# The last expert layer of a gated block: the routed tiles dealt out over three weight buffers by thirds of the sorted list

## The chip, the cores and the metric

The kernel runs on one core of a Trainium2 chip. The metric is the device time of one execution in microseconds (us). The kernel before was timed three times: the median is 1126.99 us, the lowest 1126.54 us and the highest 1131.32 us.

## The reference: what is computed

Four sequences of 512 tokens, 512 features each, run through two gated layers. Each adds an attention-like term and then an expert layer to the residual. All is done in float32. The change touches only the last of the four parts, the second layer's mixture of experts:

```
logits = x @ router_w.T                      # 2048 tokens, 8 experts
topk_w, topk_idx = top_k(softmax(logits), 2) # two experts for each token
out_e  = (silu(x @ gate_w[e]) * (x @ up_w[e])) @ down_w[e]   # 512 -> 352 -> 512
result = sum over the two chosen e of weight * out_e  +  shared expert (704 wide)
x = x + tanh(g_ffn[1]) * result              # x here is layer-normed on the way in
```

The router picks 2 of 8 experts for each of 2048 tokens, so there are 4096 (token, expert) rows. The inputs are fixed by their seed. The reference's own choice of experts gives 551, 523, 549, 483, 478, 438, 454 and 620 rows for experts 0 to 7.

## The kernel before, in words

The kernel does first layer attention, 32 small experts over 48 tiles, second layer attention, and then the part that matters here. All of it is one function, `flamingo_gated`.

**The sorted list.** In the last layer the 4096 rows are sorted by expert. Each expert's rows are padded to whole tiles of 128 rows (`P`). With the counts above that is 5, 5, 5, 4, 4, 4, 4 and 5 tiles, 36 in all, and `NTS` is 36. `NT4` is 39, the most that any routing could need; the last three would run inside a conditional (line 1537) if more than 36 were used. `tile_i` (line 935) is a small table that says which tile of the sorted list is done at which step; before the change it is simply 0, 1, 2, and so on. From it VectorE works out, for each step, the expert (`eid`, lines 1358 to 1360), the rows of the weight table to fetch (`wrow`), and the column of the slot table where the step's tokens stand (`column`, `pick4`).

**Three weight buffers.** `wbuf` holds `NW = 3` buffers. Step i uses the buffer `at4[i] % 3`, so steps i, i+3, i+6 share one. `weights4(i)` (line 1393) fetches the gate and up weights, 128 rows of 2816 floats (1.44 MB), and the down weights, 128 rows of 1536 floats (0.79 MB), with two indirect DMAs that GpSimd issues. Before it, line 1367 compares the experts of step i and step i-3:

```
V.tensor_tensor(same[:, NW:NTS], eid[:, NW:NTS], eid[:, : NTS - NW], ALU.is_equal)
...
V.scalar_tensor_tensor(wrow, same, float(4 * E1 * P), eid, ALU.mult, ALU.add)
```

Where they agree, the row numbers are pushed out of bounds, and the DMA moves nothing: the weights are in the buffer already.

**One step.** `rows4` gathers a tile's 128 token rows (steps 0 to 3), `in4` turns them with a ScalarE copy `x32` (line 1441), four TensorE transposes (line 245) and a ScalarE copy into `xrT` (line 246). From step 4 on, `pair_rows4` gathers two tiles at once into `rp`; 16 DMAs on SyncE's queue rearrange them into `q` (line 1453), and VectorE transposes them (`in4_blocks`, line 1461). `up4` does gate and up on TensorE (`pgr`, `pur`, line 1472), Silu on ScalarE (1474) and the product on VectorE (1475). `turn4` transposes the product (`pti`, 1483) and ScalarE copies it (`itr`, 1484 and 1485). `down4` does the down projection (`por`, 1492), VectorE adds half the bias (`yr`, 1494), and GpSimd scatters the rows to DRAM (1495).

**The order.** TensorE and VectorE follow the order in which the program is written (`by_hand`). TensorE's is: up(i+1), then the transposes of tile i+2 where step i+2 is below 4, then down(i), then `pti`(i+1). GpSimd, ScalarE and SyncE are ordered by the planner that compiles the kernel. After step i the program asks for `weights4(i + 3)`. The weights of steps 0 and 1 are asked for earlier (line 1398), while the shared expert of the same layer (`d1`, lines 1203 to 1229, whose weights lie in the buffer that step 2 will use) is still at work. The third, `weights4(2)`, is written after `up4(0)` and after the gathers of `pair_rows4` for tiles 4 to 7.

**After the loop.** The second part of the shared expert follows, one step of it ahead of the last down projection, and the results go out.

Of the kernel before, what the change touches and what calls it, by code (L numbers as in the profile page):

```python
# [34 lines left out]
NT4 = (2 * T + E1 * (P - 1)) // P  # L35
NTS = 2 * T // P + E1 // 2
# [6 lines left out]
NW = 3  # L43
# [22 lines left out]
def flamingo_gated(  # L66
# [9 lines left out]
    V, A, G, PE = nc.vector, nc.scalar, nc.gpsimd, nc.tensor  # L76
# [42 lines left out]
    for g in range(B):  # L119
# [23 lines left out]
        pattern=[[1, P]], channel_multiplier=-1,  # L143
# [97 lines left out]
    def transposed(dst, src, name, part=slice(0, P)):  # L241

        pt = ps_t.tile([P, DC, P], F32, name=name, tag="pt")
        for c in range(DC):
            PE.transpose(pt[:, c, :], src[:, c * P : (c + 1) * P], ident)
        A.copy(dst, pt[:, :, part])  # L246
# [15 lines left out]
    ENG = mybir.EngineType  # L262
# [441 lines left out]
    def views4(w):  # L704
        wgu = wbuf[w % NW][:, :WROW].rearrange("p (a c i) -> p a c i", a=2, c=DC)
        return wgu, wbuf[w % NW][:, WROW:].rearrange("p (c d) -> p c d", d=D)
# [7 lines left out]
    def load_shared4(u, w):  # L714
        wgu, wd = views_s4(u, w)
        nc.sync.dma_start(out=wgu, in_=(wsgu1a, wsgu1b)[u])
        nc.sync.dma_start(out=wd[:, 0:2, :], in_=wsd1[u * IS[0] :, :][: 2 * P, :].rearrange("(c p) d -> p c d", p=P))
        if u == 0:
            for h in range(2):
                nc.sync.dma_start(out=wd[h * N : (h + 1) * N, 2, :], in_=wsd1[2 * P : IS[0], :])  # L720
# [134 lines left out]
    for i in range(NT2):  # L855
# [4 lines left out]
        k = i // 4 + 2  # L860
# [50 lines left out]
    for i in range(2):  # L911
        for k in range(2):
# [3 lines left out]
                pattern=[[(g2 - g) * P, 2], [TB * P, TB]], base=1 + k * T + g * P, channel_multiplier=1,  # L916
# [15 lines left out]
    for c in range(2, DC):  # L932
        G.tensor_tensor(fold, fold, ident[:, 32 * c : 32 * c + E1], ALU.add)
    tile_i = c4.tile([P, NT4], I32, name="tile_i")
    G.iota(tile_i, pattern=[[1, NT4]], base=0, channel_multiplier=0)


    stats4 = [c4.tile([P, 3, TB], F32, name=f"st4_{g}") for g in range(B)]
# [303 lines left out]
    def step(gen, n=1):  # L1242
        for _ in range(n):
            next(gen)
# [135 lines left out]
    def gather(out_, src, idx, n):  # L1380
        G.indirect_dma_start(
            out=out_,
            out_offset=None,
            in_=src[:, :],
            in_offset=bass.IndirectOffsetOnAxis(ap=idx, axis=0),
            bounds_check=n - 1,
            oob_is_err=False,
        )
# [4 lines left out]
    def weights4(i):  # L1393
        wgu, wd = views4(at4[i])
        gather(wgu.rearrange("p a c i -> p (a c i)"), wgu1, wrow[:, i : i + 1], E1 * P)
        gather(wd.rearrange("p c d -> p (c d)"), wd1, wrow[:, i : i + 1], E1 * P)
# [37 lines left out]
    def rows4(i):  # L1434
        xrs[i] = work.tile([P, D], F32, name=f"xr{i}", tag="row", bufs=NROW)
        gather(xrs[i], h4_dram, gat4[:, i : i + 1], T)

    def in4(i):
        xrTs[i] = work.tile([P, DC, P], F32, name=f"xrT{i}", tag="xnT", bufs=3)
        x32 = work.tile([P, DC, B4, 32], F32, name=f"x32_{i}", tag="row", bufs=NROW)  # L1440
        A.copy(x32, xrs.pop(i).rearrange("p (r c d) -> p c r d", r=B4, c=DC))
        transposed(xrTs[i], x32.rearrange("p c r d -> p (c r d)"), f"ptr{i}")
# [3 lines left out]
    def pair_rows4(i):  # L1446
        rp = d4.tile([P, 2, D], F32, name=f"rp{i}", tag="rp", bufs=3)
        for j in range(2):
            gather(rp[:, j, :], h4_dram, gat4[:, i + j : i + j + 1], T)
        q = d4.tile([P, 2, B4, P], F32, name=f"q{i}", tag="q", bufs=2)  # L1450
        for a in range(B4):
            for r in range(DC):
                nc.sync.dma_start(
                    out=q[32 * r : 32 * r + 32, :, a, :], in_=rp[32 * a : 32 * a + 32, :, r * P : (r + 1) * P]
                )
        for j in range(2):
            xqs[i + j] = q[:, j]
# [8 lines left out]
    def up4(i):  # L1466
        (wgu, _), xbT = views4(at4[i]), xrTs.pop(i)
        pg = ps.tile([P, I1], F32, name=f"pgr{i}", tag="g")
        pu = ps.tile([P, I1], F32, name=f"pur{i}", tag="u")
        for a, p_ in enumerate((pg, pu)):  # L1470
            for c in range(DC):
                PE.matmul(p_, lhsT=xbT[:, c, :], rhs=wgu[:, a, c, :], start=(c == 0), stop=(c == DC - 1))  # L1472
        sg = work.tile([P, 512], F32, name=f"sgr{i}", tag="sg")
        A.activation(sg[:, :I1], pg, AF.Silu)
        V.scalar_tensor_tensor(sg[:, :I1], pu, slots[:, 1, i : i + 1], sg[:, :I1], ALU.mult, ALU.mult)  # L1475
        sgs[i] = sg

    def turn4(i, tag="it"):
        pt = ps_t.tile([P, 3, P], F32, name=f"pti{i}", tag="pt")
        it = work.tile([P, 3, P], F32, name=f"itr{i}", tag=tag)  # L1480
        sg = sgs.pop(i)
        for ic, (i0, ni) in enumerate(chunks):
            PE.transpose(pt[:ni, ic, :], sg[:, i0 : i0 + ni], ident)
        A.copy(it[:, 0:2, :], pt[:, 0:2, :])
        A.copy(it[: I1 - 2 * P, 2, :], pt[: I1 - 2 * P, 2, :])
        its[i] = it

    def down4(i):
        (_, wd), it = views4(at4[i]), its.pop(i)
        po = ps.tile([P, D], F32, name=f"por{i}", tag="o")  # L1490
        for ic, (i0, ni) in enumerate(chunks):
            PE.matmul(po, lhsT=it[:ni, ic, :], rhs=wd[:ni, ic, :], start=(ic == 0), stop=(ic == 2))  # L1492
        yr = work.tile([P, D], F32, name=f"yr{i}", tag="row", bufs=NROW)
        V.tensor_tensor(yr, po, half_db, ALU.add)  # L1494
        d = G.indirect_dma_start(  # L1495
            out=y4_dram[:, :],
            out_offset=bass.IndirectOffsetOnAxis(ap=put4[:, i : i + 1], axis=0),
            in_=yr,
            in_offset=None,
            bounds_check=2 * T - 1,  # L1500
            oob_is_err=False,
        )

        tc.declare_no_dep(d.ins, group="y4", reason="rows are distinct")
        tc.add_to_no_dep_group("y4", d.ins)

    after = [shared4(1, W5, g, wd2) for g in range(B)]
    BYPE = 4
    for i in range(BYPE):
        rows4(i)  # L1510
    for i in range(BYPE, BYPE + 4, 2):
        pair_rows4(i)
    in4(0)
    up4(0)
    weights4(NW - 1)
    in4(1)
    turn4(0)
    for i in range(NTS):
        if i + 1 < NTS:
            up4(i + 1)  # L1520
        if i + 2 < NTS:
            (in4 if i + 2 < BYPE else in4_blocks)(i + 2)
        if i % 2 == 0 and BYPE + 4 <= i + 6 < NTS:
            pair_rows4(i + 6)
        if i + 1 == NTS:
            step(after[0])
        down4(i)
        if i + NW < NTS:
            weights4(i + NW)
        elif i + NW == NTS:  # L1530
            load_shared4(1, W5)
        if i + 1 < NTS:
            turn4(i + 1)
    step(after[0], 3)
    by_hand.close()

# [109 lines left out]
```

## Time and profile before

| what | value |
| --- | --- |
| median of three runs | 1126.99 us |
| the profiled execution: own time | 1132.97 us |
| the profiled execution: span, first to last instruction | 1131.2 us |
| TensorE busy | 1016.3 us, 90% of the span |
| mean granted TensorE clock | 0.946 |
| routed steps, first gate matmul to the last step's gate matmul | 711.98 to 992.58 us |
| instructions in the span | 11060 |

The profiled execution is one run and not the median one: its own time is 1132.97 us, of which 1131.2 us are its span, so that 1.8 us lie around the span. Times in the views are from the start of the span. In a timeline a row gives the start, the busy time, the engine, the line, the operation with output and inputs and its count, and in brackets the idle time just before it with what ended that time. PE is TensorE's matmul, ACT is ScalarE, DVE is VectorE, POOL is GpSimd, and SPq is SyncE's DMA queue.

### The profile page before, as it was taken

The page shows a single profiled execution, that of the slowest core. Times are in us where ns is not written, and L with a number is a line of the kernel's source. Part 1 is how long each engine was busy: PE and PEld are TensorE (multiplying, and loading weights), DVE is VectorE, ACT ScalarE, POOL GpSimd, SP SyncE. Part 2 cuts the span into 40 slices and gives each one's busy share as a digit, 9 for nine tenths or more (in the row PEclk, how much of TensorE's full clock was granted, in tenths as well). Part 3 has the DMA queues.
Part 4 walks back from the last instruction along what each step waited for, and adds up shares of the span by engine and source line. Part 5 has one row for each costly group of instructions (what it writes and reads, how often), then busy time and mean ns, then how long its engine had stood idle before and what let it go on. Part 6 is the DMA issues. An engine that isn't in the chain of part 4 may idle for free. (4 is left out here: it accounts for less than half of the span.)

```text
span 1131.2 us, 11060 instructions
## 1 busy us (share of the span) xinstructions
PE 1016.3 (90%) x3334; PEld 495.0 (44%) x3334; DVE 466.1 (41%) x1244; ACT 212.1 (19%) x461; POOL 375.2 (33%) x412
## 2 busy tenths in 40 slices
PE   4479889999999999799486798899999999999998
PEld 2144434444444444334243444555555555544443
DVE  5989936322232322376856353122222222218111
ACT  1143111222222222023232300211111111110000
POOL 2001142334322340466624443554554544310000
PEclk8689889999999999899878599999999999999999
DMA  9522136688888786765633606697799878639100
GB/s 323 220 75 80 44 85 234 220 296 270 283 288 268 257 289 223 261 174 173 200 93 124 57 1 169 194 294 221 244 322 319 271 274 281 216 111 325 38 37 37
DMA packets 88477, 223.12 MB, mean 197 GB/s; under 512 B 21054, under 2 KB 38494, under 8 KB 80224
## 3 DMA queue, kind: packets, MB, share of 16 engines
q0 software_dynamic: 28608, 107.81, 30.3%
q1 hardware_dynamic: 57504, 110.40, 28.4%
q10 hardware_dynamic: 2304, 4.20, 1.5%
q8 instruction: 27, 0.44, 0.2%
q14 instruction: 34, 0.28, 0.1%
HBM read 206.16 MB, written 35.57 MB: 214 GB/s over the span
## 5 line engine op out<-in xcount | busy, mean ns | idle before, releaser
L788 PE MATMUL gu<-wbuf,xbT 128*128 128x512 f32 (+1 forms) x512 | 176.7, 602 | 0.9 <-ACT xbT L246 0.7
L950 POOL DMA_INDIRECT yk<-y_dram,rows_of x76 | 83.8, 1102 | 107.2 <-DVE x L967 51.2
L1472 PE MATMUL pgr<-wbuf,xrT 128*128 128x352 f32 x288 | 93.9, 470 | 11.8 <-DMA wbuf<-in_wgu_dram,wrow 8.7
L770 POOL DMA_INDIRECT xb<-h_dram,get x48 | 48.1, 1001 | 168.5 <-issue 96.9
L788 PEld LDWEIGHTS gu<-wbuf,xbT 128*128 128x128 f32 (+1 forms) x512 | 64.2, 165 | 79.4 <-issue 78.3
L1492 PE MATMUL por<-wbuf,itr 128*128 128x512 f32 (+1 forms) x216 | 98.6, 592 | 0.0
L795 DVE SCALAR_TENSOR_TENSOR sgb<-gu,xb,sgb 128x256 f32<-128x256 f32 (+1 forms) x64 | 30.9, 484 | 160.9 <-ACT sgb L793 136.7
L1475 DVE SCALAR_TENSOR_TENSOR sgr<-pur,slots,sgr 128x352 f32<-128x352 f32 x36 | 21.0, 583 | 177.7 <-PE pur L1472 126.1
L813 PE MATMUL pob<-wbuf,itb 128*128 128x512 f32 (+1 forms) x256 | 91.2, 599 | 0.0
L1472 PE MATMUL pur<-wbuf,xrT 128*128 128x352 f32 x288 | 91.1, 459 | 0.0
L1203 PE MATMUL pg<-lnT,wbuf 128*128 128x512 f32 (+1 forms) x224 | 86.0, 563 | 0.1
L1203 PE MATMUL pu<-lnT,wbuf 128*128 128x512 f32 (+1 forms) x224 | 79.6, 532 | 1.9 <-DVE it L1209 1.9
L1495 POOL DMA_INDIRECT y_dram<-yr,put x36 | 36.8, 1021 | 114.5 <-DVE yr L1494 106.0
L1472 PEld LDWEIGHTS pgr<-wbuf,xrT 128*128 128x128 f32 x288 | 52.7, 193 | 38.4 <-DVE yr L1494 9.1
L1472 PEld LDWEIGHTS pur<-wbuf,xrT 128*128 128x128 f32 x288 | 54.7, 190 | 30.5
L1219 PE MATMUL po<-wbuf,it 128*128 128x512 f32 x128 | 63.0, 627 | 4.2 <-DVE x L1229 3.3
L1492 PEld LDWEIGHTS por<-wbuf,itr 128*128 128x128 f32 (+1 forms) x216 | 41.0, 190 | 41.9 <-issue 34.7
L748 POOL DMA_INDIRECT found<-cnt_dram,look x48 | 48.3, 1006 | 26.3 <-issue 14.3
L1203 PEld LDWEIGHTS pg<-lnT,wbuf 128*128 128x128 f32 (+1 forms) x224 | 36.1, 185 | 46.3 <-issue 44.5
L1203 PEld LDWEIGHTS pu<-lnT,wbuf 128*128 128x128 f32 (+1 forms) x224 | 34.9, 175 | 42.8 <-issue 38.1
L1209 DVE SCALAR_TENSOR_TENSOR it<-pu,ub_sb,sg 128x512 f32<-128x512 f32 (+1 forms) x24 | 16.9, 703 | 85.9 <-PE pu L1203 65.3
L818 DVE COPY y<-pob 128x512 f32<-128x512 f32 x48 | 33.2, 691 | 44.7 <-PE pob L813 31.2
(397 smaller groups left out, 1288.8 us busy)
## 6 DMA issues: line engine op xcount, KB each, us to landing
wbuf<-in_wgu_dram SPq DMA_DIRECT2D x32, 1024.0 KB
wbuf<-in_wd_dram SPq DMA_DIRECT2D x32, 512.0 KB
y_dram<-y SPq DMA_DIRECT2D x48, 256.0 KB
q<-rp SPq DMA_DIRECT2D x256, 32.0 KB
y<-y_dram SPq DMA_DIRECT2D x32, 256.0 KB
lnT<-in_xT_dram SPq DMA_DIRECT2D x4, 1024.0 KB
x<-in_x_dram SPq DMA_DIRECT2D x16, 256.0 KB
h_dram<-h SPq DMA_DIRECT2D x16, 256.0 KB
```

The costliest lines, as they stand in the source:

```text
L748: G.indirect_dma_start(out=found[k][:, j, :], out_offset=None, in_=cnt_dram[:, :], in_offset=bass.IndirectOffsetOnAxis(ap=look2[:, i : i + ...
L770: G.indirect_dma_start(out=rows0[i], out_offset=None, in_=h_dram[:, :], in_offset=bass.IndirectOffsetOnAxis(ap=get2[:, i : i + 1], axis=0) ...
L788: PE.matmul(gu[p_, :], lhsT=xbT[:, c, p_], rhs=weights[e][0][:, c, :], start=(c == 0), stop=(c == DC - 1),)
L795: V.scalar_tensor_tensor(sg[p_, :I0], gu[p_, I0:], xb[p_, D + e : D + e + 1], sg[p_, :I0], ALU.mult, ALU.mult)
L813: PE.matmul(po[p_, :], lhsT=it[:, ic, p_], rhs=weights[e][1][:, ic, :], start=(ic == 0), stop=(ic == I0 // P - 1),)
L818: V.tensor_copy(y, po)
L950: G.indirect_dma_start(out=yk, out_offset=None, in_=y_dram[:, :], in_offset=bass.IndirectOffsetOnAxis(ap=rows_of[:, t, k : k + 1], axis=0) ...
L1203: PE.matmul(p_[m, :n], lhsT=wgu[:, a, c, i], rhs=lnT[g][:, c, k], start=(c == 0), stop=(c == DC - 1))
L1219: PE.matmul(po, lhsT=it[:, ic, k * P : (k + 1) * P], rhs=wd[:, ic, :] if ic < 2 else wd2, start=(ic == 0), stop=(ic == 2),)
L1472: PE.matmul(p_, lhsT=xbT[:, c, :], rhs=wgu[:, a, c, :], start=(c == 0), stop=(c == DC - 1))
L1492: PE.matmul(po, lhsT=it[:ni, ic, :], rhs=wd[:ni, ic, :], start=(ic == 0), stop=(ic == 2))
L1495: d = G.indirect_dma_start(out=y4_dram[:, :], out_offset=bass.IndirectOffsetOnAxis(ap=put4[:, i : i + 1], axis=0), in_=yr, in_offset=None, ...
```

## The change

The table `tile_i` no longer counts 0, 1, 2 and so on. Its first 36 entries are filled as a 12 by 3 block whose entry (k, w) is k + 12 w. Step 3k + w therefore does tile 12 w + k of the sorted list: the first buffer walks through tiles 0 to 11, the second through 12 to 23, the third through 24 to 35. The last three entries, of the conditional, stay 36 to 38, and take a second small instruction.

Besides this, the gathers of `pair_rows4` for tiles 4 to 7 are written after `weights4(2)`, not before `in4(0)`. And ScalarE and GpSimd follow the written order from `in4(0)` until the end of step 1 (`in_order`); afterwards the planner orders them, as before. Where such a stretch falls among instructions of the same engine that are written outside it is still the planner's choice.

```diff
-    G.iota(tile_i, pattern=[[1, NT4]], base=0, channel_multiplier=0)
+
+    G.iota(
+        tile_i[:, :NTS].rearrange("p (k w) -> p k w", w=NW), pattern=[[1, NTS // NW], [NTS // NW, NW]],
+        base=0, channel_multiplier=0,
+    )
+    G.iota(tile_i[:, NTS:], pattern=[[1, NT4 - NTS]], base=NTS, channel_multiplier=0)
@@
     for i in range(BYPE):
         rows4(i)
-    for i in range(BYPE, BYPE + 4, 2):
-        pair_rows4(i)
+    in_order = ExitStack()
+    in_order.enter_context(tc.manual_schedule(engines={ENG.Activation, ENG.Pool}))
     in4(0)
     up4(0)
     weights4(NW - 1)
+    for i in range(BYPE, BYPE + 4, 2):
+        pair_rows4(i)
     in4(1)
     turn4(0)
     for i in range(NTS):
@@
         if i + 1 < NTS:
             turn4(i + 1)
+        if i + 3 == BYPE:
+            in_order.close()
     step(after[0], 3)
```

## The prediction

> **What bounds the kernel now.** I began with the page. TensorE is busy 90% of the span, so time is gained only where TensorE waits or runs at a lower clock. The chain of waits covers only the last 113 us (from 1017.88, after the conditional), which the change doesn't touch, so I went to the stage instead. The page's busy line and the group of gate matmuls:
>
> ```profile
> PE 1016.3 (90%) x3334; PEld 495.0 (44%) x3334; DVE 466.1 (41%) x1244; ACT 212.1 (19%) x461; POOL 375.2 (33%) x412
> ...
> L1472 PE MATMUL pgr<-wbuf,xrT 128*128 128x352 f32 x288 | 93.9, 470 | 11.8 <-DMA wbuf<-in_wgu_dram,wrow 8.7
> ```
>
> Gate matmuls are where TensorE loses time in the routed steps: 11.8 us, of which 8.7 wait for gate/up weights. The busy times by stretch show where (length, then PE, PEld, DVE, ACT, POOL, granted clock, DMA share, GB/s):
>
> ```profile
> 736.05:843.11 107.06, 107.06 (x352) 62.41 (x351) 26.65 (x43) 13.94 (x42) 53.60 (x53) 1.00 0.83 275
> ...
> 859.57:992.58 133.01, 124.72 (x401) 71.60 (x401) 29.82 (x48) 15.40 (x46) 60.33 (x60) 1.00 0.78 271
> ```
>
> From step 3 to step 17 TensorE never stops: 107.06 / 14 = 7.647 us a step (7.643 between neighbours). Later it is short of work by 8.3 us. TensorE's timeline, gate matmuls alone, steps 17 to 19, 22 and 23:
>
> ```profile
> 843.11 2.60 PE L1472 MATMUL pgr<-wbuf,xrT 128*128 128x352 f32 x8
> 850.83 2.53 PE L1472 MATMUL pgr<-wbuf,xrT 128*128 128x352 f32 x8
> 859.57 2.60 PE L1472 MATMUL pgr<-wbuf,xrT 128*128 128x352 f32 x8 [0.94 <-DMA wbuf<-in_wgu_dram,wrow]
> ...
> 884.16 2.53 PE L1472 MATMUL pgr<-wbuf,xrT 128*128 128x352 f32 x8
> 893.46 2.60 PE L1472 MATMUL pgr<-wbuf,xrT 128*128 128x352 f32 x8 [1.49 <-DMA wbuf<-in_wgu_dram,wrow]
> ```
>
> From step 17 (843.11) to step 34 (984.94) are 141.83 us, against 17 x 7.643 = 129.93: 11.9 us lost. GpSimd's timeline says why the early loads cost nothing and the late ones do:
>
> ```profile
> 836.25 1.02 POOL L1495 DMA_INDIRECT y_dram<-yr,put  x1 [1.37 <-issue]
> 837.58 1.01 POOL L1381 DMA_INDIRECT wbuf<-in_wd_dram,wrow  x1 [0.31 <-issue]
> 838.89 1.00 POOL L1381 DMA_INDIRECT wbuf<-in_wgu_dram,wrow  x1 [0.30 <-issue]
> ...
> 851.67 1.02 POOL L1495 DMA_INDIRECT y_dram<-yr,put  x1 [2.81 <-DVE yr L1494]
> 853.00 1.02 POOL L1381 DMA_INDIRECT wbuf<-in_wgu_dram,wrow  x1 [0.31 <-issue]
> ```
>
> Counting requests, the one at 838.89 is step 18's (used at 850.83, 11.9 us later), the one at 853.00 is step 19's, stuck behind the scatter of step 16 and used 6.6 us later, after a wait. Up to step 18 a request leads by 9 to 12 us; from 19 to 32 it comes after the scatter.
>
> The second place is the start. ScalarE's timeline, then TensorE's:
>
> ```profile
> 708.03 0.62 ACT L1441 COPY x<-xr 128x512 f32<-128x512 f32 x1 [10.68 <-DMA xr<-h_dram,gat]
> 709.49 0.62 ACT L1441 COPY x<-xr 128x512 f32<-128x512 f32 x1 [0.83 <-DMA xr<-h_dram,gat]
> 710.82 0.62 ACT L1441 COPY x<-xr 128x512 f32<-128x512 f32 x1 [0.72 <-DMA xr<-h_dram,gat]
> 711.34 0.58 ACT L246 COPY xrT<-ptr 128x512 f32<-128x512 f32 x1
> ```
>
> ```profile
> 708.71 0.66 PE L245 MATMUL ptr<-ident,x 128*128 128x128 f32 x4
> 711.98 4.33 PE L1472 MATMUL pgr<-wbuf,xrT 128*128 128x352 f32 x8 [2.61 <-ACT xrT L246]
> ```
>
> The transposes of tile 0 end at 709.37, but ScalarE first serves tiles 1 and 2, waiting for their rows. TensorE idles 2.61 us, and its first eight gate matmuls take 4.33 instead of 2.53 us: the granted clock is 0.50 from 712 to 715.
>
> **What the Trainium skill says.** "TensorE: Matmul & The Clock Gate", Part 1: the array falls to half clock after about one idle window of 3.4 us and needs about 3.4 us of work to return. The trace agrees in kind (some 3.4 us at half clock), though here 2.61 us of idleness sufficed; idle 0.5 to 1.5 us (697.4, 893.46) left the clock at 1.00. "DMA: Bandwidth & Descriptors", section on the anatomy of a SWDGE DMA: 2.0 us + bytes/436e3. An estimate from it for 1.44 MB is 5.3 us; the trace shows 6.6 to 7.1 from request to use. The same page, SWDGE vs HWDGE vs iDMA: only one software queue is allocated; the trace too shows a single software queue for all that GpSimd issues. No page prices an indirect DMA whose rows are all out of bounds.
>
> **Part 1, the new order of tiles.** Before, a run of n tiles of one expert costs min(3, n) loads: 5,5,5,4,4,4,4,5 tiles give 8 x 3 = 24 loads, at steps 0-2, 5-7, 10-12, 15-17, 19-21, 23-25, 27-29, 31-33. That is 24 x 2.23 = 53 MB. The stalls (steps 19 on) sit on these steps. With thirds (first tiles of the experts: 0, 5, 10, 15, 19, 23, 27, 31) buffer 0 changes expert at its tiles 5 and 10, buffer 1 at tiles 15, 19, 23, buffer 2 at 27 and 31: loads at steps 0, 1, 2 and at 15, 30; 10, 22, 34; 11, 23. Ten loads, 22 MB. A load still has the same lead as before, since step i+3 is asked for after step i, so no wait gets longer by itself.
>
> Skipped loads cost no wait: steps 22, 26 and 30, skipped before, were asked for as late as 5 to 7 us ahead (946.96 for use at 951.96) and stalled nothing. GpSimd still issues 72 requests, about 1.0 us each.
>
> What remains: if GpSimd keeps its order, loads 10, 11, 15 and 34 are asked for early (34 as its request was in the trace: 972.12 for 984.94) and cost nothing. Loads 22, 23, 30 are late. First loads of a run cost 1.10, 1.66, 1.34, 1.32 us (steps 19, 23, 27, 31), mean 1.35; second ones 1.07, 0.33, 0.66, 1.02 (20, 24, 28, 32), mean 0.77. So 1.35 + 0.77 + 1.35 = 3.5 us stay, and 11.9 - 3.5 = 8.4 us are gained. Bounds: all 11.9 (no load late) and 11.9 - 5 x 1.35 - 2 x 0.77 = 3.6 (all seven late). I take the middle because the planner doesn't know which loads are skipped, so its order should stay alike.
>
> Tables: one more iota (0.165 us the one in the trace, at 427.7, nobody waits). The table arithmetic is the same instructions. Sorted position only permutes the gathered and scattered rows: bytes unchanged.
>
> **Part 2, ScalarE in written order.** `xrT`(0) follows `x32`(0): it starts when the transposes end, 709.4, takes 0.58, and the gate matmuls start at about 710.05 rather than 711.98: 1.9 us. Idle is then 0.7 us, so the clock should hold: 4.33 - 2.53 = 1.8 us more. Together 3.7; bounds 0 (the planner puts something else between) and 3.7; I take 3.7. The copies of tiles 1 to 3 come after Silu of the step before; each is needed only after that step's up matmuls (2.5 us later), so they hide there.
>
> **Part 3, the third load.** It needs `d1`'s last read of its buffer (707.47 + 1.13 = 708.6) and GpSimd free of the four `rows4` gathers (709.4): request at 709.7 instead of 714.95, 5.2 us sooner. No wait is shown before step 2 (727.96), so this gains nothing by itself; it keeps it safe, for step 2 now comes at 724.3. Behind it on GpSimd queue the four `rp` gathers, issued 2.6 us later (712.3 to 717.3), and in the one queue behind 2.23 MB (5.7 us at the 390 GB/s of 718 to 724). Rows for tiles 4, 5 land near 719.5, not 715; 16 rearranging DMAs at 0.6 us on SyncE's queue end near 729.5, landed by 731.5. VectorE wants them for tile 4 at 741.55 - 3.7 = 737.8. Cover: 6 us; without it each us late is one on TensorE. In the ordered stretch the request of step 3 goes behind the scatter of step 0, but both it and step 4's are skipped loads: nothing.
>
> **Sum.** 8.4 + 3.7 = 12.1 us. Against the profiled execution: 1132.97 - 12.1 = 1120.9. That one ran 6.0 us above the median, and no view says where; taking the same 12.1 off the median gives 1126.99 - 12.1 = 1114.9, predicted as 1115. If the median run stalls less, the gain is smaller, which the range's upper part covers.
>
> **Rivals.** (a) *All loads late, or part 2 empty*: the planner's other order on GpSimd leaves 3.6 + 3.7 = 7.3 us, or ScalarE keeps its detour and 8.4 remain: 1118.6 to 1119.7. For: the order flipped at step 19 for no visible reason. Against: seven loads, four of them where requests led by 9 us or more. (b) *Stalls mostly belong to the profiled execution*: if the median lacks its 6 us just there, 3.7 + about 2.5 = 6.2 are gained or less: 1121 to 1123, about no change. (c) *Slower: the ordered stretch ahead of the rows.* The planner may set the stretch's six requests on GpSimd (third load, four `rp` gathers) before the four `rows4` gathers. The stretch can't begin before 708.6, so rows are issued at 708.6 + 6 x 1.3 = 716.4 instead of 704.5, 11.9 us later, behind the last 1.05 MB of `rp` (2.7 us at 390 GB/s): the first step comes 14.6 us later than now, and against the 8.4 us of part 1 that is 1127 + 6.2 = 1133. It makes the kernel slower once the rows come over 8.4 us late. Against: the rows' indices are ready at 704, the load's buffer only at 708.6, so an order by readiness puts the rows first.
>
> **How the numbers follow.** Forecast (10.5 to 15.6 us gained) 0.55; (a) 0.27; (b) 0.09; (c) 0.09. Low end: 11.9 + 3.7 = 15.6 gives 1111.4, 1111. High end 1122, which takes in (a) and the better half of (b). Faster by over 0.5% (5.6 us, about what a measurement of this kernel tells from none) 0.82, within 0.09, slower 0.09. The likeliest's own range is 1111 to 1117.
>
> **What would show it.** The DMA bytes of the software queue fall by 14 x 2.23 = 31 MB from 107.81; gate matmuls wait for weights at steps 22, 23, 30 if anywhere; 36 steps near 7.64 us; first gate matmul 0.7 us after the transposes and at full clock; the load at 709.7. Wrong if gate matmuls wait for skipped loads, if `xrT` of tile 4 waits for `q`, or if the rows of tile 0 land after the third load.

## The result, and the profile after

The changed kernel takes 1118.47 us (median of six runs, 1116.55 to 1121.43) against 1127.13 us for the kernel before: a ratio of 0.9918, with a 95% interval from 0.9896 to 0.994. That is 8.7 us. The forecast was 1115 with a range of 1111 to 1122.

The profiled execution took 1118.96 us, 1117.3 of them its span. TensorE is busy for 1011.2 us, 91% of the span. The page of the changed kernel, its software DMA queue and its group of gate matmuls (line 1477 is the former 1472):

```profile
q0 software_dynamic: 28608, 76.63, 23.1%
...
L1477 PE MATMUL pgr<-wbuf,xrT 128*128 128x352 f32 x288 | 91.6, 461 | 6.8 <-DMA wbuf<-in_wgu_dram,wrow 6.1
```

The software queue moved 76.63 MB instead of 107.81, and 31.2 MB is what fourteen loads of 2.23 MB hold: 24 loads have become ten. The number of packets stayed at 28608. But gate matmuls still wait 6.1 us for weights, in four places only. TensorE's timeline of the changed kernel, gate matmuls alone, steps 14, 15, 21 to 23, 29 and 30:

```profile
810.76 2.53 PE L1477 MATMUL pgr<-wbuf,xrT 128*128 128x352 f32 x8
819.58 2.60 PE L1477 MATMUL pgr<-wbuf,xrT 128*128 128x352 f32 x8 [1.01 <-DMA wbuf<-in_wgu_dram,wrow]
...
865.51 2.53 PE L1477 MATMUL pgr<-wbuf,xrT 128*128 128x352 f32 x8
874.96 2.60 PE L1477 MATMUL pgr<-wbuf,xrT 128*128 128x352 f32 x8 [1.65 <-DMA wbuf<-in_wgu_dram,wrow]
883.50 2.60 PE L1477 MATMUL pgr<-wbuf,xrT 128*128 128x352 f32 x8 [0.66 <-DMA wbuf<-in_wgu_dram,wrow]
...
929.43 2.53 PE L1477 MATMUL pgr<-wbuf,xrT 128*128 128x352 f32 x8
940.07 2.61 PE L1477 MATMUL pgr<-wbuf,xrT 128*128 128x352 f32 x8 [2.83 <-DMA wbuf<-in_wgu_dram,wrow]
```

The steps are four of the seven that bring a new expert after the start; steps 10, 11 and 34 do not wait. Against 7.643 us a step, 1.18 us are lost before step 15, 1.81 before 22, 0.90 before 23 and 3.00 before 30; from step 3 to step 34 it is 7.1 us in all, against 12.0 in the kernel before. GpSimd's timeline at steps 15 and 30:

```profile
811.60 1.03 POOL L1500 DMA_INDIRECT y_dram<-yr,put  x1 [2.66 <-DVE yr L1499]
812.94 1.02 POOL L1386 DMA_INDIRECT wbuf<-in_wgu_dram,wrow  x1 [0.31 <-issue]
...
931.75 1.03 POOL L1500 DMA_INDIRECT y_dram<-yr,put  x1 [5.46 <-issue]
933.08 1.01 POOL L1386 DMA_INDIRECT wbuf<-in_wgu_dram,wrow  x1 [0.31 <-DMA q<-rp]
```

Both requests stand behind the scatter of three steps earlier, and are used 6.6 and 7.0 us later. At step 15 this is new: the kernel before still asked early there, at 818.60, ahead of the scatter of step 12 at 820.96. At step 30 the scatter itself was late: its input, `yr` of step 27, was ready at 929.30 + 0.69 = 929.99, and the scatter began 1.8 us after that, where 0.28 us are usual, for no reason that the trace shows.

The start has the forecast form. ScalarE's timeline, then TensorE's:

```profile
702.30 0.62 ACT L1446 COPY x<-xr 128x512 f32<-128x512 f32 x1 [14.18 <-DMA xr<-h_dram,gat]
703.67 0.59 ACT L246 COPY xrT<-ptr 128x512 f32<-128x512 f32 x1 [0.75 <-PE ptr L245]
```

```profile
702.98 0.66 PE L245 MATMUL ptr<-ident,x 128*128 128x128 f32 x4
704.31 2.63 PE L1477 MATMUL pgr<-wbuf,xrT 128*128 128x352 f32 x8 [0.68 <-ACT xrT L246]
```

TensorE idles 0.68 us instead of 2.61, and its first eight gate matmuls take 2.63 us instead of 4.33.

**Where the 8.7 us are.** From the first gate matmul to that of step 35 the changed kernel takes 274.05 us, the kernel before 280.60: 6.55 us, of which 1.7 are the first step at full clock and 4.9 the weights. With the 1.93 us of idleness ahead of it this makes 8.5 us. The two spans differ by 13.9 us. The rest lies earlier: tile 0's transposes began at 702.98 instead of 708.71, and most of this difference had come up by TensorE's 2001st matmul (659.8 and 664.3 us), in code that the change doesn't alter. Over all profiled executions shown here the transposes begin anywhere between 700.0 and 708.7 us. So spans are not compared below. The measure is the idle time before the first gate matmul plus the stretch from there to step 35's: 283.2 us before, 274.7 after.

### The profile page after: what moved, and what is told of

Its sections match the earlier page's. It is cut to its first block, busy times and chain, and to the rows that moved or that the text cites. A ratio compares the mean times of both kernels' runs of the same rounds, so it can differ in the third digit from the quotient of the medians.

```text
span 1117.3 us, 11055 instructions
## 1 busy us (share of the span) xinstructions
PE 1011.2 (91%) x3334; PEld 493.0 (44%) x3334; DVE 466.6 (42%) x1244; ACT 212.4 (19%) x461; POOL 376.4 (34%) x413
## 3 DMA queue, kind: packets, MB, share of 16 engines
q0 software_dynamic: 28608, 76.63, 23.1%
## 5 line engine op out<-in xcount | busy, mean ns | idle before, releaser
L955 POOL DMA_INDIRECT yk<-y_dram,rows_of x76 | 84.5, 1111 | 106.3 <-DVE x L972 50.1
L1477 PE MATMUL pgr<-wbuf,xrT 128*128 128x352 f32 x288 | 91.6, 461 | 6.8 <-DMA wbuf<-in_wgu_dram,wrow 6.1
```

Source lines behind the costliest of these rows:

```text
L955: G.indirect_dma_start(out=yk, out_offset=None, in_=y_dram[:, :], in_offset=bass.IndirectOffsetOnAxis(ap=rows_of[:, t, k : k + 1], axis=0) ...
```

## The experiments

The theory at this point: the thirds save late loads, ScalarE's written order saves 3.6 us at the start, and what remains is due to requests that GpSimd issues behind a scatter. Its rivals: the whole gain belongs to the ordered start; or a load is too slow whenever it is asked for.

### The tile order alone

Only the tile table is changed; the rest is the kernel before.

```diff
-    G.iota(tile_i, pattern=[[1, NT4]], base=0, channel_multiplier=0)
+    G.iota(tile_i[:, :NTS].rearrange("p (k w) -> p k w", w=NW), pattern=[[1, NTS // NW], [NTS // NW, NW]], ...)
+    G.iota(tile_i[:, NTS:], pattern=[[1, NT4 - NTS]], base=NTS, channel_multiplier=0)
```

> The kernel before with only the tile table of the change: thirds of the sorted list, one per buffer; ScalarE and GpSimd stay with the planner, the gathers for tiles 4 to 7 stay ahead of the third load. Theory (two separate gains: fewer late weight loads, and ScalarE's order at the start): the 2.6 us idle before the first gate matmul and its half clock stay; gate matmuls wait for weights only at some of the steps 10, 11, 15, 22, 23, 30, 34; first to last gate matmul 280.6 - 4.9 = about 275.7 us (273 to 278); about 4 to 5 us faster than before, 1122.5. Rival (the tile order is worth nothing, as each load has the same lead as before, and the whole gain comes with the ordered start): no faster than before, 1127, stage about 280 us. Rival (the fall in DMA traffic speeds up other stages too): 1118 or less.

Measured: 0.994 of the kernel before (0.9917 to 0.9964), the stretch 275.0 us. Gate matmuls waited at steps 22, 23 and 30 (1.54, 1.44, 3.22 us lost), and step 31 came 1.77 us late. Step 15 did not wait: its request still went out ahead of the scatter of step 12 (813.09 and 815.46). The tile order alone gives most of the change's gain, and as far as the intervals tell perhaps all of it; the rival that it is worth nothing falls.

But the start was not the one expected. TensorE's timeline of this kernel:

```profile
706.07 0.66 PE L245 MATMUL ptr<-ident,x 128*128 128x128 f32 x4
708.17 2.63 PE L1477 MATMUL pgr<-wbuf,xrT 128*128 128x352 f32 x8 [1.44 <-ACT xrT L246]
...
943.18 4.30 PE L1477 MATMUL pgr<-wbuf,xrT 128*128 128x352 f32 x8 [3.05 <-DMA wbuf<-in_wgu_dram,wrow]
```

ScalarE made the same detour over tiles 1 and 2 as in the kernel before, but here the transposes came later relative to the rows, TensorE idled only 1.44 us, and the clock held. The detour's price is thus not a fixed 3.7 us: here it was 0.8 (1.44 against 0.68). Of the kernel before only one execution was profiled, so what it pays there as a rule isn't known. The last row is step 30's: 3.05 us of idleness, and then half clock, which is the 1.77 us seen at step 31.

### The ordered start alone, and ScalarE's part of it

The first kernel is the changed one with the old tile table. The second is the kernel before with ScalarE alone in written order, from `in4(0)` to the end of step 1:

```diff
+    in_order = ExitStack()
+    in_order.enter_context(tc.manual_schedule(engines={ENG.Activation}))
     in4(0)
...
+        if i + 3 == BYPE:
+            in_order.close()
```

> The changed kernel with the old tile table (24 loads): only the ordered start of ScalarE and GpSimd and the earlier third load. Theory: idle before the first gate matmul 0.7 us instead of 2.6 (1.9 us), its first eight at full clock (1.7 us); gate matmuls wait for weights as before, about 11 us lost over the late steps; 3.6 us faster than before, 1123.5. Rival (the whole gain is here): 1118.5. Rival (the order of GpSimd for later steps shifts with it): stage loss outside 9 to 14 us.

> The kernel before with only ScalarE in written order from the first tile's copies to the end of step 1; GpSimd with the planner, tile table old, third load behind the gathers for tiles 4 to 7. Theory (the earlier third load gains nothing): the same 3.6 us as with the whole ordered start, 1123.5, and no wait for weights before step 2, though step 2 now comes 3.6 us sooner. Rival (the earlier third load is needed once the start is faster): a wait of 1 us or more before step 2's gate or down matmuls, 1124.5 or more.

Measured: 0.9999 (0.9978 to 1.002) for the ordered start, 0.9987 (0.997 to 1.0005) for ScalarE alone. Both missed the expected 3.6 us, although both begin as the changed kernel does (0.68 us idle, 2.63 us for the first eight). The loss by weights rose: from step 3 to step 34 it is 15.1 and 13.7 us, against 12.0 in the kernel before. TensorE's timeline of the first, gate matmuls of steps 15 to 18, and GpSimd's, the scatter of step 12 and the request of step 15:

```profile
820.10 2.60 PE L1472 MATMUL pgr<-wbuf,xrT 128*128 128x352 f32 x8 [1.60 <-DMA wbuf<-in_wgu_dram,wrow]
828.73 2.60 PE L1472 MATMUL pgr<-wbuf,xrT 128*128 128x352 f32 x8 [0.74 <-DMA wbuf<-in_wgu_dram,wrow]
837.00 2.60 PE L1472 MATMUL pgr<-wbuf,xrT 128*128 128x352 f32 x8 [0.40 <-DVE yr L1494]
844.72 2.53 PE L1472 MATMUL pgr<-wbuf,xrT 128*128 128x352 f32 x8
```

```profile
811.53 1.02 POOL L1495 DMA_INDIRECT y_dram<-yr,put  x1 [2.67 <-DVE yr L1494]
812.86 1.01 POOL L1381 DMA_INDIRECT wbuf<-in_wgu_dram,wrow  x1 [0.31 <-issue]
```

A whole triple of loads, steps 15 to 17, now waits which had waited for nothing before. (At step 17 the view names `yr`, that of step 15, which ended just then. It isn't the cause: step 18 begins at 844.72 without a wait, though `yr` of step 16 runs until 845.28.) With the start in written order, the planner's choice for GpSimd turns to the late pattern at step 15, not at 19. So in these profiles the ordered start gains 3.6 us in front and loses 3.1 more than before 120 us later.

In the second kernel GpSimd still turns at step 19. It loses 0.54, 1.46 and 2.14 us at steps 17, 28 and 29, where the kernel before lost 0, 0.66 and 1.01, and a little less than it at some others. Step 17's request went out ahead of the scatter and led by 9.9 us, and still its weights came late. GpSimd's timeline, then TensorE's:

```profile
823.13 1.00 POOL L1381 DMA_INDIRECT wbuf<-in_wgu_dram,wrow  x1 [0.30 <-issue]
```

```profile
833.00 2.60 PE L1472 MATMUL pgr<-wbuf,xrT 128*128 128x352 f32 x8 [0.38 <-DMA wbuf<-in_wgu_dram,wrow]
```

While this triple was loaded, from 812 to 829 us, the DMA engines were busy all the time and moved 369 GB/s. How long a load takes is thus not fixed: over all profiles, gate matmuls that waited for weights began 6.6 to 9.9 us after the request, and all times above 8 us belong to loads right behind another load. Why the kernel before lost nothing at step 17, with a lead of 9.2 us, stays open. The earlier third load had nothing to save: neither kernel waits for weights at step 2.

### Asking early, and asking late

Two kernels have GpSimd in written order throughout the routed steps. In the early one the gate/up weights are asked for ahead of the pair gathers and the scatter, in the late one after the scatter as in the program text. The early one's edit:

```diff
+        if i + NW < NTS:
+            up_weights4(i + NW)
         if i % 2 == 0 and BYPE + 4 <= i + 6 < NTS:
             pair_rows4(i + 6)
...
         if i + NW < NTS:
-            weights4(i + NW)
+            down_weights4(i + NW)
```

> The changed kernel with GpSimd in written order throughout the routed steps: gate/up weights of step i+3 are asked for ahead of the gathers and the scatter of step i, the down weights after it. Theory (what is left of the loss is that a request stands behind a scatter): every request leads by 10 to 12 us, no gate matmul waits for weights at 10, 11, 15, 22, 23, 30 or 34, first to last gate matmul 267 us instead of 274.05; 7 us faster than the changed kernel, 1111.5. Rival (a load itself is too slow, above all the second of a pair): waits of 0.5 to 1.5 us stay at steps 11 and 23, stage 269 to 271, 1114 to 1116. Rival (an early request takes bandwidth or queue room from the gathered rows): VectorE waits for q, stage 274 or more, no faster.

> The changed kernel with GpSimd in written order throughout, both weight requests of step i+3 after the scatter of step i. Theory (each real load asked for after the scatter costs 0.8 to 1.8 us): all seven steps 10, 11, 15, 22, 23, 30, 34 wait, 5 x 1.4 + 2 x 0.9 = 8.8 us and up to 1.7 more at step 30, stage 276 to 278 us against 274.05. Rival (the waits come from bandwidth that other transfers take): steps 10, 11 and 34 still wait for nothing, stage 274.

The early order measured 0.9869 of the kernel before (0.9834 to 0.9904), and the stretch 266.96 us. Its busy times by stretch, and GpSimd's timeline from the scatter of step 19 on, in which the requests at 865.50 and 866.82 are for the down weights of step 22 and the gate/up weights of step 23:

```profile
725.75:970.33 244.58, 244.58 (x802) 142.82 (x801) 60.60 (x97) 31.85 (x96) 124.61 (x123) 1.00 0.52 158
```

```profile
864.17 1.02 POOL L1505 DMA_INDIRECT y_dram<-yr,put  x1 [3.98 <-DVE yr L1504]
865.50 1.02 POOL L1386 DMA_INDIRECT wbuf<-in_wd_dram,wrow  x1 [0.31 <-DMA q<-rp]
866.82 1.00 POOL L1386 DMA_INDIRECT wbuf<-in_wgu_dram,wrow  x1 [0.30 <-issue]
```

The request of step 23 now stands ahead of the scatter of step 20. TensorE is busy for every one of 244.58 us at full clock. From step 3 to step 34 the loss is 0.01 us. Nothing waits for weights, the close pairs 10 and 11, 22 and 23 included: step 23 is asked for at 866.82 and begins at 878.61, 11.8 us later.

The late order measured 0.995 (0.9931 to 0.9969), and the stretch 279.38 us. All seven real loads wait: 2.15 us lost at step 10, 0.69 at 11, 1.20 at 15, 1.70 at 22, 1.73 at 23, 3.30 at 30 and 1.32 at 34, 12.1 in all, of the 12.4 from step 3 to step 34 (8.8 to 10.5 were expected). Steps 10, 11 and 34 never waited in the changed kernel. GpSimd's timeline, the scatter of step 7 and the request of step 10, and TensorE's, step 10:

```profile
770.74 1.04 POOL L1500 DMA_INDIRECT y_dram<-yr,put  x1 [3.98 <-DVE yr L1499]
772.09 1.01 POOL L1386 DMA_INDIRECT wbuf<-in_wgu_dram,wrow  x1 [0.31 <-issue]
```

```profile
779.69 2.60 PE L1477 MATMUL pgr<-wbuf,xrT 128*128 128x352 f32 x8 [1.98 <-DMA wbuf<-in_wgu_dram,wrow]
```

The two orders differ only in where the gate/up requests stand, so it is the place behind the scatter that costs, and the rival that steps 10, 11 and 34 wait for nothing falls. Traffic still has a part in the size: steps 11 and 23, right behind another load, began 8.3 and 8.9 us after their requests, the other five 6.7 to 7.6 us.

### The old tile order under both requests

> The early-request order of GpSimd with the old tile table (24 loads, three of 2.23 MB in consecutive steps). Theory (lead is what counts): every request leads by 10 us or more, three loads in 23 us need 6.7 MB in 23 us, 290 GB/s, which the DMA gave in this stage: no or nearly no wait, stage 267 to 268 us, as fast as the early order with thirds. Rival (the number of loads counts even when they are early): the third load of each triple is late by 1 us or more, 7 us in all, stage 274.

> The same late order with the old tile table (24 loads, 21 after the start). Theory: all seven triples cost what the four late ones cost before, 2.9 us each, 20 us in all, stage 287 us; thirds are then worth 10 to 11 us. Rival (a load's price is not fixed by its request): stage 281 as before.

Both are the two orders above with the old tile table, 24 loads. The early one measured 0.9874 (0.9831 to 0.9916), the stretch 266.97 us, 0.01 us apart from that with thirds. Its TensorE, DMA and throughput while the triples of steps 5, 10 and 15 were loaded, in the busy times by stretch:

```profile
726.00:850.00 124.00, 124.00 (x406) 72.13 (x405) 30.38 (x48) 15.93 (x48) 64.62 (x64) 1.00 0.84 279
```

The DMA carried 279 GB/s, 84% of its engines' time, and TensorE lost nothing. In the late one all seven triples lost time: 19 of their 21 steps waited, and steps 6 and 11 were late by 1.77 and 1.76 us because the clock had fallen to half after the waits before steps 5 and 10 (1.85 and 2.29 us). From step 3 to step 34 it lost 27.3 us, the stretch was 294.25 us (287 were expected), and the one run took 1136.11 us.

### The changed kernel again, beside these

> The changed kernel itself, on this chip, beside the others. Expected as measured: stage 274 us, waits at steps 15, 22, 23 and 30; 0.992 of the kernel before; slower than the early order with thirds by some 6 us.

Measured 0.9932 (0.9908 to 0.9956), the stretch 276.06 us. Its waits are those of steps 15, 22, 23 and 30 again; the 2.0 us more are step 31, late by 1.77 us, after a wait of 2.97 us at step 30, 2.83 in the first profile. The eight gate matmuls of step 30 took 4.30 us instead of 2.61: the granted clock was 0.50 from 942 to 945 us. So two profiles of one kernel can differ by 2 us in this measure.

The experiments ran on two chips, each kernel beside the kernel before (medians 1130.56 and 1128.17 us there), and the ratios are to that. All together, with idle time before the first gate matmul plus stretch, and each kernel's loss from step 3 to step 34 (us):

| kernel | loads | idle + stretch | loss, steps 3 to 34 | ratio to the kernel before |
| --- | --- | --- | --- | --- |
| before | 24 | 283.2 | 12.0 | 1 |
| ordered start alone | 24 | 282.7 | 15.1 | 0.9999 |
| ScalarE's order alone | 24 | 281.3 | 13.7 | 0.9987 |
| tile order alone | 10 | 276.4 | 8.0 | 0.994 |
| changed kernel, both profiles | 10 | 274.7, 276.7 | 7.1, 9.1 | 0.9918, 0.9932 |
| asked late, thirds | 10 | 280.1 | 12.4 | 0.995 |
| asked late, old order | 24 | 294.9 | 27.3 | one run only |
| asked early, old order | 24 | 267.6 | 0.01 | 0.9874 |
| asked early, thirds | 10 | 267.6 | 0.01 | 0.9869 |

In these profiles the thirds are worth 15 us with late requests, of which 3.5 are half clock, and nothing with early ones. The early order is quicker than the kernel before by 1.3% and quicker than the changed kernel with either tile table, by 7 to 9 us in the profiles and by 5 to 7 us from the ratios.

## Why the prediction was right

**Direction and size.** The time of 1118.47 us lies in the range of 1111 to 1122, 3.5 us above the predicted 1115; 8.7 us were gained of 12.1. It lies outside the 1111 to 1117 that the prediction called the likeliest, between these and rival (a). The mechanism, fewer late loads and a start without the detour, shows in the profile, and the term that was mis-sized is part 1.

**Part 1, "3.5 us stay, and 8.4 us are gained".** Measured: 7.1 us stay and 4.9 are gained (9.1 and 2.9 in the second profile, where 1.8 us are half clock). The count of ten loads and their steps was right, as the 31.2 MB and the seven waits of the late order show. The step that failed is "if GpSimd keeps its order": the ordered start moved the planner's turn to late requests from step 19 to step 15, which cost 1.18 us there. The price of a late load was too low besides: 1.81 and 0.90 us for the pair, where 1.35 and 0.77 stood, and 3.00 for step 30, where a scatter that began 1.8 us late came on top. The lower bound of 3.6 us was made for all seven late; the late order lost 12.4 us, so that bound was too favourable. The same holds for the 6.6 to 7.1 us from request to use: the loads waited for in the prediction's own trace took 6.6 to 7.8, and up to 9.9 elsewhere.

**"A load still has the same lead as before"** was right for the program text and wrong as a reason: the lead that counts is made by GpSimd's order, and this was free to move.

**Part 2, 1.9 and 1.8 us.** In the profiles 1.93 and 1.7. Yet by itself the ordered start gained nothing measurable: in its profile 3.1 us were lost again, as GpSimd's turn moved. With the tile order alone and the planner's ScalarE, TensorE idled 1.44 us and the clock stayed full, so the 3.6 us may not be there to save in every execution of the kernel before. How much part 2 gives in the median of the changed kernel is thus not shown.

**Part 3, nothing.** Right: step 2 waits in none of the kernels, with or without the earlier load, and VectorE's transposes for tile 4 held up no gate matmul. One reading in its working was off: from 718 to 724 us the DMA moved 359 GB/s and not 390, so that the third load takes about 0.5 us more of the 6 us of cover.

**The 6.0 us of the profiled execution above the median.** Most likely they lie ahead of the routed steps: TensorE's 2001st matmul began at 664.3 us there and at 656.7 to 662.3 in the other nine profiles. This is read from other kernels, as no second execution of the kernel before was profiled; it speaks against rival (b) and for taking the same sum off the median. Rival (a), with 7.3 to 8.4 us, came closest to the 8.7 measured, but by another mix: some loads late and, in the profile, part 2 in full. Rival (c) did not occur: the `rows4` gathers went ahead of the third load (698.82 to 703.74, and 704.04).

**Skipped loads cost nothing**: no skipped step waited for its weights in any kernel; step 31's delay in two of them was the clock.

## What to carry to other kernels

When an engine waits for a load, look first at what stands ahead of the request on the engine that issues it; here moving one request ahead of a scatter took away every wait, and the number of loads was then of no account. Removing transfers helped here only where they were late, and where a planner orders the issuing engine, a small edit elsewhere can change which these are. A gain at one place must be checked against the whole stretch: the ordered start's 3.6 us were there in the trace, and 120 us later 3.1 us of them were gone again.

## What the runs showed of the hardware that was not expected

How long TensorE idles does not by itself decide whether the clock falls to half. In TensorE's timelines of these kernels, idle times of 1.85, 2.29, 2.61, 2.97 and 3.05 us were followed by 1.7 to 1.8 us of loss at half clock; 1.44, 1.90, 1.98, 2.83 and 3.12 us (the last asked late, thirds, step 30) were not. What matters is how the idle time lies in fixed windows. In each of the ten traces every change of the granted clock falls on one grid of 3.413 us. From tile 0's transposes to step 35, TensorE idled 1.85 us or more in five windows of these grids (1.85, 2.29, 2.69, 2.97 and 3.05 us), and the window after each ran at half clock; in all others it idled at most 1.79 us, and the clock held. Busy times in two neighbouring windows at step 30, of the changed kernel's second profile and then of the late order with thirds:

```profile
938.39:941.80 3.41, 0.44 (x3) 0.30 (x2) 0.54 (x1) 0.53 (x2) 2.80 (x3) 1.00 1.02 391
941.80:945.21 3.41, 3.41 (x7) 2.03 (x6) 0.00 (x0) 0.00 (x0) 1.16 (x2) 0.50 0.98 342
```

```profile
936.51:939.92 3.41, 1.73 (x7) 0.71 (x5) 0.82 (x2) 0.53 (x2) 2.60 (x3) 1.00 0.97 381
939.92:943.34 3.42, 1.98 (x7) 1.37 (x8) 0.00 (x0) 0.00 (x0) 2.46 (x3) 1.00 0.98 341
```

In the first, 2.97 us of idleness lie in one window. In the second, the longer 3.12 us are split over two, 1.68 and 1.44. This border belongs to the routed steps: elsewhere, with other matmuls, 1.40 us in a window were followed by half clock (the early order, 71.93 us) and 1.97 were not (553.21 us). The Trainium skill's page "TensorE: Matmul & The Clock Gate", Part 1, calls the window free-running and gives it 3413 ns, which the grid bears out; the page lets the clock fall after a whole idle window, while here about half a window of idleness sufficed.

The weight requests that skip all rows left the packet count of the software queue at 28608 while its bytes fell by 31.2 MB. In what time such a request completes wasn't measured by itself; the shortest lead seen without a wait was 4.1 us, at step 3 of both late orders. Why GpSimd begins late at one place of its program stays open: in all eight profiles but those of the early orders the scatter of step 27 began 1.75 us after its input was ready, where 0.28 us are usual, and in the two early orders GpSimd idled 1.4 us before the weight request of step 30 instead, where nothing came of it. It is always the 390th or 391st instruction that the profile counts on GpSimd.
